# Normed tokens of the last six chunks written to DRAM and read back in squares of 32; VectorE transposes them instead of TensorE

## The chip, the core and the metric

The kernel runs on one core of a Trainium2 chip. The metric is the device time in microseconds of that core, as a median over runs. The profile shows one profiled execution.

## What is computed

The input is 2 sequences of 2048 tokens with 256 values each, all in float32. Two layers follow each other, each on normed tokens and added to its input:

```python
x = x + attention(layernorm(x))      # W_write, W_read, decay, log_alpha
x = x + mixture_of_experts(layernorm(x))

# attention: 4 heads of 64; causal, linear, with decay; the keys are the reads one token later
v  = y @ W_write.T;  rk = y;  wk = y moved down by one token
read = decay_part * (W_state @ rk) + ((rk @ wk.T) * M) @ v     # chunk by chunk
W_state = g_C * W_state + (v * g_w).T @ wk
out = y + (alpha * read) @ W_read.T

# experts: 8, the best 2 of each token by softmax, each 256 -> 1024 (gelu) -> 256
```

So a token of the attention is needed in three forms: normed, with tokens across the partitions (for the sums); transposed, with the 256 values across the partitions (`yT`, for the products); and moved by one token (`wk`, the keys).

## The kernel before, in words

**Chunks.** Each sequence is cut into 16 chunks of 128 tokens; a chunk holds both sequences. The attention walks over chunks p = 0 to 15 (`attention(p)`, here called pass p), each in seven steps with a yield between them. The order of instructions on every engine is the order in which this program writes them (a manual schedule); each engine runs its own list in order, SP (SyncE) too, which issues nearly all transfers. A transfer on SP that has to wait stops the transfers behind it.

**What a chunk passes through.** `norm_stats(p)` (L291) and `norm(p)` compute the normed tokens `y` two passes ahead: `norm(p + 2)` is the end of step 4 of pass p. Up to chunk 10 ACT writes `y` (L311), later VectorE (L315). Then `wk` is loaded from `y` on chip: its first row from the chunk before (L323), and the rest in two transfers of 112 and 15 rows (L324, L325). After that `load_x` (L98) asks for a later chunk of x. `transposes(p + 1)` stands in step 4 of pass p: four transposes by TensorE (L355) into the PSUM tile `pt` of 128x512, and a copy by ACT (L361) into `yT`, whose column 0 is the last token of the chunk before (L360). The tile `pt` shares its one PSUM buffer with `pK` of the routing (L627). Pass p itself opens with `pv` (L428) and `pS` (L437), which read `yT`; VectorE multiplies `pS` by the decay mask into `A` (L443), and `wk` by `g_w` into `wkg` (L382). Later in the pass come `pR` (L480, L488) with ACT's copy `rdT` (L493), then ACT's `sums` (L336), then `pW` (L508), which VectorE adds into the state (L513), then `rg` (L368) and `norm(p + 2)`. The result of the pass before (`pO`, L406, added by L409) is written by SP to `out` (L413).

**Experts beside it.** From pass 9 on, pieces of the second layer's work lie between the steps. A tile is 128 or 256 rows of one expert, and a piece is one eighth of its 1024 hidden values: `ph` (L894), gelu by ACT into `hT` (L899), and, three pieces later, `py` (L850). Which pieces stand after which step is fixed by `pieces_by`. `pv`, `pO`, `pW` and `ph` share three PSUM buffers of the tag "pm". A tile needs its rows `xg` from the slots in DRAM (L791, four transfers, in squares of 32 tokens), the numbers `wn` (L797), a bias `b2c` (L775) and 1 MB of weights `w1c` (L777); SP issues them one to three tiles ahead, with three buffers each (four for `b2c`). VectorE turns `xg` into `xT` by its transpose of squares of 32 (L821). At the end of a tile VectorE writes `yo` (L861) and POOL adds it to `out` (L864).

**Routing.** Every second pass a group of 512 tokens is routed in small VectorE instructions that are strewn between the others (L561 to L649), with four ACT instructions `payload` (L566) that need VectorE's shift (L252), two TensorE products `pK` (L627, L629), and POOL's writes of rows to the slots (L536).

Of the kernel before, what the change touches and what calls it, by code (L numbers as in the profile page):

```python
# [10 lines left out]
F32 = mybir.dt.float32  # L11
I32 = mybir.dt.int32
AF = mybir.ActivationFunctionType
ALU = mybir.AluOpType
# [4 lines left out]
P = 128  # L19
B, T, D = 2, 2048, 256  # L20
# [3 lines left out]
NC = T // P  # L24
# [6 lines left out]
S = 32  # L31
Q = P // S
# [28 lines left out]
def block_kernel(  # L61
# [12 lines left out]
    b2: bass.AP,  # L74
    out: bass.AP,
    slots: bass.AP,
):
    nc = tc.nc

# [2 lines left out]
    chk = ctx.enter_context(tc.tile_pool(name="chk", bufs=2))  # L82
# [13 lines left out]
    def load_x(p):  # L96
        xin = chk.tile([P, B, D], F32, tag="xin", name=f"xin_{p}", bufs=4)
        nc.sync.dma_start(xin, x.rearrange("b t d -> t b d")[p * P : (p + 1) * P])  # L98
        return xin
# [70 lines left out]
    g_w = one([P, H], F32, "g_w")  # L170
# [99 lines left out]
                return  # L270

    ys, wks, yTs, x1s, ups, stats2, rgs, wkgs = {}, {}, {}, {}, {}, {}, {}, {}
    shifts, vs, rdTs = {}, {}, {}
    EASY = 9
    BUSY = 8
    LATE = 7
    mark = {}
# [2 lines left out]
    def group_tiles(q):  # L280
        if q not in x1s:
            x1s[q] = grp.tile([P, G, D + E], F32, tag="x1", name=f"x1_{q}")
            stats2[q] = grp.tile([P, G, 2], F32, tag="mv2", name=f"mv2_{q}")
        return x1s[q], stats2[q]
# [13 lines left out]
    def norm(p):  # L298

        xin = xins[p]  # L300
        mv, ve, rstd = ups[p]
        shift = shift_of(mv[:, :, 0], rstd, B, f"a{p}")
        ups[p] = (mv, ve, rstd)
        beside()
        up = sml.tile([P, B], F32, tag="up", name=f"up_{p}")
        nc.vector.tensor_scalar(up, rstd, 1.0, None, ALU.add)
        shifts[p] = (shift, up)
        y = chk.tile([P, B, D], F32, tag="y", name=f"y_{p}", bufs=3)
        for b in range(B):
            if 1 < p < EASY + 2:  # L310
                nc.scalar.activation(  # L311
                    y[:, b, :], xin[:, b, :], AF.Identity, bias=shift[:, b : b + 1], scale=rstd[:, b : b + 1]
                )
            else:
                nc.vector.tensor_scalar(  # L315
                    y[:, b, :], xin[:, b, :], rstd[:, b : b + 1], shift[:, b : b + 1], ALU.mult, ALU.add
                )

        wk = chk.tile([P, B, D], F32, tag="wk", name=f"wk_{p}")
        if p == 0:  # L320
            nc.gpsimd.memset(wk[0:1, :, :], 0.0)
        else:
            nc.sync.dma_start(wk[0:1, :, :], ys[p - 1][127:128, :, :])  # L323
        nc.sync.dma_start(wk[1:113, :, :], y[0:112, :, :])  # L324
        nc.sync.dma_start(wk[113:128, :, :], y[112:127, :, :])  # L325
        ys[p], wks[p] = y, wk
        if p + 2 < NC:
            xins[p + 2] = load_x(p + 2)

    def sums(p):  # L330

# [17 lines left out]
    def transposes(p):  # L349

        yT = chk.tile([P, B, 2, P + 1], F32, tag="yT", name=f"yT_{p}")
        pt = ps_t.tile([P, B, 2, P], F32, tag="pt", name=f"pt_{p}")
        for b in range(B):
            for c in range(2):
                nc.tensor.transpose(pt[:, b, c, :], ys[p][:, b, c * P : (c + 1) * P], ident)  # L355
        if p == 0:
            nc.gpsimd.memset(yT[:, :, :, 0:1], 0.0)
            nc.vector.tensor_copy(yT[:, :, :, 1:], pt)  # L358
        else:
            nc.scalar.copy(yT[:, :, :, 0:1], yTs[p - 1][:, :, :, P : P + 1])  # L360
            nc.scalar.copy(yT[:, :, :, 1:], pt)  # L361
        yTs[p] = yT

    def scaled_reads(p):

# [7 lines left out]
    def scaled_writes(p):  # L373
        if p < NC - 1:
            wkg = chk.tile([P, B, H, HD], F32, tag="wkg", name=f"wkg_{p}", bufs=1)
            wk = wks[p].rearrange("p b (h d) -> p b h d", h=H)
            if p < EASY:
                for h in range(H):
                    nc.scalar.activation(wkg[:, :, h], wk[:, :, h], AF.Identity, scale=g_w[:, h : h + 1])
            else:  # L380
                for b in range(B):
                    nc.vector.tensor_tensor(  # L382
                        wkg[:, b], wk[:, b], g_w.unsqueeze(2).to_broadcast([P, H, HD]), ALU.mult
                    )
            wkgs[p] = wkg
# [32 lines left out]
    def attention(p):  # L418


        q, at = p // 2, 2 * (p % 2)
        first, last = p == 0, p == NC - 1
        x1, _ = group_tiles(q)
        yT = yTs[p]
        for b in range(B):
# [21 lines left out]
        beside()  # L447
        if p + 2 < NC and p < EASY:
            norm_stats(p + 2)
# [9 lines left out]
        if not last:  # L459
            transposes(p + 1)  # L460
        if p + 2 < NC and p >= EASY:
            norm_stats(p + 2)
# [21 lines left out]
        for b in range(B):  # L484
            for hh in range(2):
                for j in range(2):
                    hs = slice((2 * hh + j) * HD, (2 * hh + j + 1) * HD)
# [9 lines left out]
        for b in range(B):  # L497
            if p < EASY:
                nc.scalar.activation(x1[:, at + b, D:], vs[b][:, D:], AF.Identity, scale=std1[:, b : b + 1])
            else:  # L500
                nc.vector.tensor_scalar(x1[:, at + b, D:], vs[b][:, D:], std1[:, b : b + 1], None, ALU.mult)
        if not last:
            pW = ps_m.tile([P, B, 2, HD], F32, tag="pm", name=f"pW_{p}")
            for b in range(B):
                for hh in range(2):
                    for j in range(2):
                        h = 2 * hh + j
# [471 lines left out]
    for p in range(NC):  # L979
        for k, _ in enumerate(attention(p)):  # L980
            if p == 0 and k == 0:
                behind_first()
            if (p or k > 3) and k in (0, 2, 3, 4, 5) and halves < W2_BY[p]:
                e, j = divmod(halves, 2)
# [91 lines left out]
```

## Time and profile before

| | |
|---|---|
| median of 3 runs | 623.9 us (622.66 to 626.26) |
| the profiled execution's own time | 626.45 us |
| its span, first to last instruction | 624.7 us |
| mean granted TensorE clock | 0.990 |
| TensorE transposes, L355 | 64, of which 24 for chunks 10 to 15 |
| wk transfers, L323, L324, L325 | 15, 16 and 16 |
| TensorE starts on the transposes of chunks 10 to 15 | 103.65, 126.69, 150.83, 179.93, 210.39, 245.59 us |

The span is the time from the first to the last instruction of the program; the device time of the same execution is 1.7 us longer. A row of the timeline reads: start, duration, engine, line, operation, what it writes and reads, form, count, and in brackets the idle time of the engine before it and what ended it. Rows marked "q" are the engine's sequencer, which issues transfers; a transfer's row is the time of its issue, not of its landing. A row of a table by windows reads: stretch, its length, busy time and number of instructions of each engine, the granted TensorE clock as a share of full speed, the busy share of the 16 DMA engines, and GB/s. Matmuls are pipelined, so how long a group holds TensorE is read from the start of the next group. q1 is the queue of SP's transfers; its row gives packets, megabytes, and the share of the time of 16 DMA engines.

### The profile page before, as it was taken

The page shows a single profiled execution, that of the slowest core. Times are in us where ns is not written, and L with a number is a line of the kernel's source. Part 1 is how long each engine was busy: PE and PEld are TensorE (multiplying, and loading weights), DVE is VectorE, ACT ScalarE, POOL GpSimd, SP SyncE. Part 2 cuts the span into 40 slices and gives each one's busy share as a digit, 9 for nine tenths or more (in the row PEclk, how much of TensorE's full clock was granted, in tenths as well). Part 3 has the DMA queues.
Part 4 walks back from the last instruction along what each step waited for, and adds up shares of the span by engine and source line. Part 5 has one row for each costly group of instructions (what it writes and reads, how often), then busy time and mean ns, then how long its engine had stood idle before and what let it go on. Part 6 is the DMA issues. An engine that isn't in the chain of part 4 may idle for free. (4 is left out here: it accounts for less than half of the span.)

```text
span 624.7 us, 12845 instructions
## 1 busy us (share of the span) xinstructions
PE 603.0 (97%) x3864; PEld 529.3 (85%) x3864; DVE 249.3 (40%) x1039; ACT 240.7 (39%) x586; POOL 223.6 (36%) x199
## 2 busy tenths in 40 slices
PE   7998879999999999999999999999999999999995
PEld 6876758888888888888888888888888899999995
DVE  4787876567345534452255111221111132222220
ACT  6686673352333332422232222222222234444442
POOL 3216655546315622455266222222222121221121
PEclk9998998999999999999999999999999999999999
DMA  4799595679645366446657676466445568777742
GB/s 133 232 341 325 161 278 158 167 213 247 163 109 131 89 149 149 110 115 168 141 122 196 158 180 134 93 130 127 118 101 136 140 182 206 194 199 227 208 107 28
DMA packets 88856, 102.53 MB, mean 164 GB/s; under 512 B 52576, under 2 KB 77024, under 8 KB 83152
## 3 DMA queue, kind: packets, MB, share of 16 engines
q1 hardware_dynamic: 75360, 84.03, 46.8%
q0 software_dynamic: 12720, 17.47, 15.3%
q8 instruction: 35, 0.57, 0.4%
q14 instruction: 37, 0.30, 0.2%
q10 hardware_dynamic: 704, 0.14, 0.1%
HBM read 74.41 MB, written 23.01 MB: 156 GB/s over the span
## 5 line engine op out<-in xcount | busy, mean ns | idle before, releaser
L894 PE MATMUL ph<-xT,w1c 128*128 128x256 f32 (+1 forms) x1408 | 294.3, 332 | 5.7 <-issue 4.8
L850 PE MATMUL py<-w_sb,hT 128*128 x1072 | 288.8, 380 | 0.0
L899 ACT ACTIVATE hT<-ph,b1c 128x256 f32<-128x256 f32 (+1 forms) x352 | 148.4, 422 | 322.3 <-PE ph L894 293.6
L894 PEld LDWEIGHTS ph<-xT,w1c 128*128 128x128 f32 x1408 | 240.6, 192 | 34.6 <-issue 5.1
L864 POOL DMA_INDIRECT out<-yo,dest x67 | 105.2, 1570 | 291.1 <-DVE yo L861 196.1
L850 PEld LDWEIGHTS py<-w_sb,hT 128*128 128x128 f32 x1072 | 191.3, 191 | 19.2
L861 DVE SCALAR_TENSOR_TENSOR yo<-py,wt,b2c 128x256 f32<-128x256 f32 x67 | 30.3, 481 | 249.9 <-PE py L850 249.9
L536 POOL DMA_INDIRECT slots<-pay,slot_i x64 | 63.3, 989 | 62.2 <-issue 30.6
L428 PE MATMUL pv<-wwg,yT 128*128 128x264 f32 x128 | 33.9, 411 | 1.5 <-DVE yT L358 1.5
L406 PE MATMUL pO<-wrg,rdT 128*128 128x264 f32 x128 | 34.2, 401 | 0.0
L443 DVE TENSOR_TENSOR A<-pS,dmask 128x1024 f32<-128x1024 f32 x16 | 19.6, 1223 | 35.9 <-PE pS L437 28.8
L428 PEld LDWEIGHTS pv<-wwg,yT 128*128 128x128 f32 x128 | 24.4, 198 | 5.9 <-DVE yT L358 1.7
L406 PEld LDWEIGHTS pO<-wrg,rdT 128*128 128x128 f32 x128 | 24.0, 194 | 4.6 <-ACT v L430 0.2
L821 DVE STREAM_TRANSPOSE xT<-xg 128x512 f32<-128x512 f32 (+1 forms) x44 | 25.4, 576 | 0.2 <-issue 0.2
L836 DVE TENSOR_SCALAR b2c<-b2c,wt 128x256 f32<-128x256 f32 x67 | 23.8, 356 | 2.4
L409 DVE TENSOR_TENSOR x<-x,pO 128x264 f32<-128x264 f32 x32 | 13.4, 426 | 20.2 <-PE pO L406 20.2
L488 PE MATMUL pR<-A,v 128*64 128x128 f32 x256 | 18.0, 279 | 2.9 <-issue 2.2
L247 POOL TENSOR_TENSOR rstd_a<-ve_a,expo 128x2 f32<-128x2 f32 x16 | 11.6, 723 | 25.2 <-DVE ve_a L245 13.7
L566 ACT ACTIVATE pay<-x,shift_b,rstd_b 128x256 f32<-128x256 f32 x32 | 19.0, 593 | 3.8 <-DVE shift_b L252 3.7
L437 PEld LDWEIGHTS pS<-yT 64*128 64x128 f32 x256 | 15.5, 187 | 5.8 <-issue 3.7
L488 PEld LDWEIGHTS pR<-A,v 128*64 128x64 f32 x256 | 13.9, 136 | 6.0 <-issue 4.9
L437 PE MATMUL pS<-yT 64*128 64x128 f32 x256 | 18.6, 284 | 0.0
(161 smaller groups left out, 392.5 us busy)
## 6 DMA issues: line engine op xcount, KB each, us to landing
w1c<-in_w SPq DMA_DIRECT2D x44, 1024.0 KB
w_sb<-in_w SPq DMA_DIRECT2D x16, 512.0 KB
xg<-slots SPq DMA_DIRECT2D x92, 64.0 KB
b2c<-in_b SPq DMA_DIRECT2D x44, 128.0 KB
out<-x SPq DMA_DIRECT2D x16, 256.0 KB
xin<-in_x SPq DMA_DIRECT2D x15, 256.0 KB
wk<-y SPq DMA_DIRECT2D x16, 224.0 KB
xg<-slots SPq DMA_DIRECT2D x84, 32.0 KB
```

Source lines behind the costliest of these rows:

```text
L406: nc.tensor.matmul(pO, lhsT=rdTs[p][:, c, b * P : (b + 1) * P], rhs=wrg[:, c, :], start=(c == 0), stop=(c == 1))
L428: nc.tensor.matmul(pv, lhsT=yT[:, b, c, 1:], rhs=wwg[:, c, :], start=(c == 0), stop=(c == 1))
L437: nc.tensor.matmul(pS[:, j, (2 * b + hh) * P : (2 * b + hh + 1) * P], lhsT=yT[r, b, hh, 0:P], rhs=yT[r, b, hh, 1:], start=True, stop=True,)
L488: nc.tensor.matmul(pR[half(j, hh), hh, b * P : (b + 1) * P], lhsT=vs[b][:, hs], rhs=A[:, j, b, hh * P : (hh + 1) * P], start=(first and b ...
L536: put = nc.gpsimd.indirect_dma_start(out=next(slot_views), out_offset=IndirectOffsetOnAxis(ap=index, axis=0), in_=rows, in_offset=None,)
L821: nc.vector.transpose(xT.rearrange("p c (i s) -> p c i s", s=S), xg.rearrange("p i (c s) -> p c i s", s=S))
L836: nc.vector.tensor_scalar(b2c[:, j], b2c[:, 0], wt[:, j : j + 1], None, ALU.mult)
L850: nc.tensor.matmul(r["py"][:, j * D : (j + 1) * D], lhsT=hT[:, j * SB : (j + 1) * SB], rhs=w2_sb[:, ds(r["at"], 1), fc * D : (fc + 1) * D] ...
L861: nc.vector.scalar_tensor_tensor(yo, r["py"][:, j * D : (j + 1) * D], r["wt"][:, j : j + 1], r["b2c"][:, j], ALU.mult, ALU.add)
L864: add = nc.gpsimd.indirect_dma_start(out=next(out_views), out_offset=IndirectOffsetOnAxis(ap=r["dest"][:, j : j + 1], axis=0), in_=yo, in_ ...
L894: nc.tensor.matmul(ph, lhsT=r["w1c"][:, c, fc * P : (fc + 1) * P], rhs=r["xT"][:, c, :], start=(c == 0), stop=(c == 1),)
L899: mark[0] = nc.scalar.activation(hT, ph, AF.Gelu_apprx_tanh, bias=r["b1c"][:, fc : fc + 1]).ins.name
```

## The change

From chunk 10 on (the eleventh), `norm(p)` writes `y` with its 256 values in another order (squares of 32 interleaved), and SP writes it to a new DRAM tensor `normed`. At the start of the pass before the chunk's own, the new function `squares(p)` reads it back twice: as `wk`, rows 0 to 126 into partitions 1 to 127 in one transfer, and its first row from the chunk before (for chunk 10, in four small transfers from `y` of chunk 9 on chip); and as `yg`, in four transfers, one for each 32 partitions, so that each square of 32 tokens by 32 values lies where VectorE's transpose of squares turns it into its part of `yT`. `transposes(p)` then is two VectorE transposes of 128x256 instead of TensorE's four and ACT's copy. `yg` takes its buffers from the tag of `y`. `scaled_writes` reads `wk` in the new order, in four VectorE instructions of 128x128 instead of two of 128x256.

```diff
--- before.py
+++ after.py
@@ -74,6 +74,7 @@
     b2: bass.AP,
     out: bass.AP,
     slots: bass.AP,
+    normed: bass.AP,
 ):
     nc = tc.nc
 
@@ -270,8 +271,9 @@
                 return
 
     ys, wks, yTs, x1s, ups, stats2, rgs, wkgs = {}, {}, {}, {}, {}, {}, {}, {}
-    shifts, vs, rdTs = {}, {}, {}
+    shifts, vs, rdTs, ygs = {}, {}, {}, {}
     EASY = 9
+    SQUARE = 10
     BUSY = 8
     LATE = 7
     mark = {}
@@ -307,15 +309,21 @@
         shifts[p] = (shift, up)
         y = chk.tile([P, B, D], F32, tag="y", name=f"y_{p}", bufs=3)
         for b in range(B):
+            at = by_square(y[:, b]) if p >= SQUARE else y[:, b]
+            of = xin[:, b].rearrange("p (c k s) -> p c k s", c=2, s=S) if p >= SQUARE else xin[:, b]
             if 1 < p < EASY + 2:
                 nc.scalar.activation(
-                    y[:, b, :], xin[:, b, :], AF.Identity, bias=shift[:, b : b + 1], scale=rstd[:, b : b + 1]
+                    at, of, AF.Identity, bias=shift[:, b : b + 1], scale=rstd[:, b : b + 1]
                 )
             else:
                 nc.vector.tensor_scalar(
-                    y[:, b, :], xin[:, b, :], rstd[:, b : b + 1], shift[:, b : b + 1], ALU.mult, ALU.add
+                    at, of, rstd[:, b : b + 1], shift[:, b : b + 1], ALU.mult, ALU.add
                 )
 
+        ys[p] = y
+        if p >= SQUARE:
+            nc.sync.dma_start(normed[p].rearrange("(b t) d -> t b d", b=B), y)
+            return next_x(p)
         wk = chk.tile([P, B, D], F32, tag="wk", name=f"wk_{p}")
         if p == 0:
             nc.gpsimd.memset(wk[0:1, :, :], 0.0)
@@ -323,9 +331,37 @@
             nc.sync.dma_start(wk[0:1, :, :], ys[p - 1][127:128, :, :])
         nc.sync.dma_start(wk[1:113, :, :], y[0:112, :, :])
         nc.sync.dma_start(wk[113:128, :, :], y[112:127, :, :])
-        ys[p], wks[p] = y, wk
+        wks[p] = wk
+        next_x(p)
+
+    def next_x(p):
         if p + 2 < NC:
             xins[p + 2] = load_x(p + 2)
+
+    def by_square(t):
+
+        return t.rearrange("p (k c s) -> p c k s", c=2, s=S)
+
+    def squares(p):
+
+
+        wk = chk.tile([P, B, D], F32, tag="wk", name=f"wk_{p}")
+        nc.sync.dma_start(wk[1:P], normed[p].rearrange("(b t) d -> t b d", b=B)[: P - 1])
+        if p > SQUARE:
+            nc.sync.dma_start(wk[0:1], normed[p - 1].rearrange("(b t) d -> t b d", b=B)[P - 1 : P])
+        else:
+            for b in range(B):
+                for c in range(2):
+                    nc.sync.dma_start(
+                        by_square(wk[0:1, b])[:, c],
+                        ys[p - 1][P - 1 : P, b, c * P : (c + 1) * P].rearrange("p (k s) -> p k s", s=S),
+                    )
+        wks[p] = wk
+        yg = chk.tile([P, B * Q, 2, S], F32, tag="y", name=f"yg_{p}", bufs=3)
+        rows = normed[p].rearrange("(j s) (k d) -> s j k d", s=S, k=Q)
+        for k in range(Q):
+            nc.sync.dma_start(yg[k * S : (k + 1) * S].rearrange("p j c s -> p j (c s)"), rows[:, :, k, :])
+        ygs[p] = yg
 
     def sums(p):
 
@@ -349,6 +385,16 @@
     def transposes(p):
 
         yT = chk.tile([P, B, 2, P + 1], F32, tag="yT", name=f"yT_{p}")
+        yTs[p] = yT
+        if p >= SQUARE:
+            nc.scalar.copy(yT[:, :, :, 0:1], yTs[p - 1][:, :, :, P : P + 1])
+            yg = ygs.pop(p)
+            for b in range(B):
+                nc.vector.transpose(
+                    yT[:, b, :, 1:].rearrange("p c (i s) -> p c i s", s=S),
+                    yg[:, b * Q : (b + 1) * Q].rearrange("p i c s -> p c i s"),
+                )
+            return
         pt = ps_t.tile([P, B, 2, P], F32, tag="pt", name=f"pt_{p}")
         for b in range(B):
             for c in range(2):
@@ -359,7 +405,6 @@
         else:
             nc.scalar.copy(yT[:, :, :, 0:1], yTs[p - 1][:, :, :, P : P + 1])
             nc.scalar.copy(yT[:, :, :, 1:], pt)
-        yTs[p] = yT
 
     def scaled_reads(p):
 
@@ -377,6 +422,15 @@
             if p < EASY:
                 for h in range(H):
                     nc.scalar.activation(wkg[:, :, h], wk[:, :, h], AF.Identity, scale=g_w[:, h : h + 1])
+            elif p >= SQUARE:
+                for b in range(B):
+                    for c in range(2):
+                        hs = slice(2 * c, 2 * c + 2)
+                        nc.vector.tensor_tensor(
+                            wkg[:, b, hs].rearrange("p h (k s) -> p h k s", s=S),
+                            by_square(wks[p][:, b])[:, c].rearrange("p (h k) s -> p h k s", h=2),
+                            g_w[:, hs].unsqueeze(2).unsqueeze(3).to_broadcast([P, 2, 2, S]), ALU.mult,
+                        )
             else:
                 for b in range(B):
                     nc.vector.tensor_tensor(
@@ -420,6 +474,8 @@
 
         q, at = p // 2, 2 * (p % 2)
         first, last = p == 0, p == NC - 1
+        if SQUARE <= p + 1 < NC:
+            squares(p + 1)
         x1, _ = group_tiles(q)
         yT = yTs[p]
         for b in range(B):
...
```

## The prediction

> **What bounds the kernel now.** I read the page's busy times first, then the order of instructions on TensorE and on SP around the changed chunks, then the gaps of TensorE.
>
> ```profile
> PE 603.0 (97%) x3864; PEld 529.3 (85%) x3864; DVE 249.3 (40%) x1039; ACT 240.7 (39%) x586; POOL 223.6 (36%) x199
> ...
> PEclk9998998999999999999999999999999999999999
> ...
> q1 hardware_dynamic: 75360, 84.03, 46.8%
> ```
>
> TensorE is busy 97% of the span at nearly full clock; no other engine passes 40%. From 160 us on it has no idle time at all, so each microsecond of TensorE work removed there is one off the end, and each new stall is one on it. What one group of transposes is worth is read from starts, since ends overlap (timeline, TensorE):
>
> ```profile
> 179.06 1.03 PE L850 MATMUL py<-w_sb,hT 128*128 x4
> 179.93 0.60 PE L355 MATMUL pt<-ident,y 128*128 128x128 f32 x4
> 180.36 1.03 PE L894 MATMUL ph<-xT,w1c 128*128 128x256 f32 x4
> ```
>
> The four transposes hold TensorE for 180.36 - 179.93 = 0.43 us (109 ns each), not the 0.60 printed. A gap costs more than its length (timeline, then busy time by windows):
>
> ```profile
> 94.40 2.05 PE L894 MATMUL ph<-xT,w1c 128*128 128x128 f32 x8 [4.80 <-issue]
> ```
>
> ```profile
> 94.40:98.00 3.60, 3.60 (x12) 3.19 (x13) 2.28 (x13) 1.66 (x4) 3.60 (x2) 0.50 0.70 189
> ```
>
> After 4.80 us of idleness the next 3.6 us ran at a granted clock of 0.50 (column PEclk): another 1.8 us lost. SP's transfers around pass 10 (the attention of chunk 10, which must fetch chunk 11):
>
> ```profile
> 120.19 0.09 SPq L777 DMA_DIRECT2D w1c<-in_w  x1
> 122.27 0.47 SPq L777 DMA_DIRECT2D w1c<-in_w  x1
> 123.81 2.08 SPq L791 DMA_DIRECT2D xg<-slots  x4
> 126.08 1.77 SPq L797 DMA_DIRECT2D wn<-slots  x1
> 127.98 1.44 SPq L413 DMA_DIRECT2D out<-x  x1
> ```
>
> `squares(11)` will stand, in program order, between the wn of 126.08 and the out of 127.98, behind two 1 MB loads. By the trace's completion records the second of these is complete at 131.9 and the wn at 133.2. But TensorE transposed chunk 11 at 126.69, before SP would even have issued its read.
>
> **The change, part by part.** *Removed:* 6 x 4 transposes, 6 x 0.43 = 2.6 us of TensorE, all on the path. Six ACT copies of 0.585 us (L361), beside other work: nothing.
>
> *Added on VectorE:* 12 transposes; nearest row, L821 at 128x256, 436 ns: 0.8 us a chunk. `wkg` in four pieces instead of two of 418 ns: +0.3 us. The strided y writes have no row; nothing to +0.4 us, I take nothing, as float32 rows stay 128-byte runs. VectorE is busy 13.8 of 20 us at 120:140, so about 1.1 us a chunk lies in its idle time, if nothing makes it wait.
>
> *Queues.* SP issues per chunk: three wk transfers (0.57 + 0.54 + 0.90 us) become one write (0.45, as L98), a wk read, its first row (four small ones for chunk 10) and four yg reads (0.5 each, as L791). The chain write, next x, weights, read begins about 1.0 to 1.4 us earlier and is 3 us longer (4.5 at chunk 10) past the read; the xg, w1c behind it are used 8 us and more later, so that alone costs nothing. No POOL issue moves, but its adds wait for yo, which wait with VectorE. The write waits for y as L324 did; the read waits for it to land, about 2 us (out at 91.83 lands 94.1), always over by then.
>
> *The wk read.* It now moves 127 rows of 2 x 1 KB in one transfer, where the kernel before has 112 + 15. Row first: of q1's 75,360 packets, the data rows of the transfers listed on the page make 68,704; the 6,656 left are completion posts, and 417 SP transfers at 16 each would be 6,672. The 16 missing are one for each of the sixteen 15-row transfers: the rows set how many DMA engines a transfer uses. This trace can't say what 127 does. The Trainium skill, "DMA: Bandwidth & Descriptors", section "Why a DMA increments its semaphore by 16 and not by 1", can: the largest number up to 16 that divides the slowest dimension, and 127 rows go to one engine. Spread over 16 the read takes 254 x 46 ns / 16 = 0.7 us (46 ns is the trace's median for a 1 KB packet on q1); on one it takes 11.7 us (10.4 at the 24.9 GB/s that an engine moves when the share is 1.0; an estimate of 13 with POOL's packets of 102 ns between). And the engine is a queue: a sixteenth of each later transfer waits behind it, so yg too is complete only then. I take one engine, 11.7.
>
> *The new wait.* VectorE stops at its transposes until yg has landed (T). Behind it stand the statistics, gate factors, shift of the routing, the state update (L513), y of the next chunk. TensorE gets 3 buffers of tag "pm": pW takes one that L513 frees, so the third `ph` after pW waits for it; in pass 10 ACT waits too, as the first `payload` (L566) needs the shift (L252).
>
> Pass 9: SP reaches the slot at 97.1 (98.5 less 1.4). Data from 98.3, wk to 110.0, yg's 64 packets of 18 ns on that engine 1.2, completion 0.6: T = 111.8. VectorE's turn is 105.5. L513 ends T + 0.8 + 2.9 (L291 to L501) + 0.5 = 116.0; the third ph was due at 111.27 - 0.44 = 110.8. Stall 5.2, and 1.8 of clock: 7.0.
>
> Pass 10: y of chunk 11 is ready 1.5 later, 117.5. From there to the slot SP took 15.2 (112.6 to 127.9), less 1.0: 131.7; the weights before it are complete 4.0 on, 135.7; wk 11.7, yg 1.8: T = 149.2. ACT's gelu of the second piece after pW ends at T + 4.9 (transposes 0.8, L291 to L252 1.6, payload, rdT and sums 2.1, gelu 0.4); TensorE was due to need it at 134.69 - 0.9 + 7.0 = 140.8. Stall 13.3, and about 1.2 of clock, ACT being the limit at first: 14.5.
>
> Pass 11: y at T + 4.8 = 154.0; SP's chain 13.8 - 1.0: 166.8; weights complete 5.5 later, 172.3; wk and yg: T = 185.8. L513 ends T + 4.7 = 190.5; the third ph is due at 159.54 - 1.3 + 21.5 = 179.7. Stall 10.8 and 1.8: 12.6.
>
> Pass 12: T = 217.3 by the same steps, L513 at 220.5, the third ph due at 220.2: nil. Passes 13 and 14: SP reaches the slot 16 and 9 us ahead of the turn even now, and the third ph comes 10 us after it: nil, 1.6 us short of a stall in the last.
>
> Sum: 7.0 + 14.5 + 12.6 - 2.6 = 31.5 us; three gaps of the trace before (0.29, 0.56, 0.40 us at 111 to 156) should vanish in the stalls: 30.5. The profiled execution took 626.45 us (span 624.7), 2.5 above the median of 623.9; its rows carry over to the median: 623.9 + 30.5 = 654.
>
> **Rivals.** *1. The read is spread over 16 engines* (the split of 112 + 15 was for another reason). Then pass 9 has no stall (T = 103, turn 105.5). In pass 10 the read still stands behind the two w1c loads: complete 131.9 - 1.4, xg, wk, yg and completion 4.0: T = 134.5. Gelu at 139.4, due 133.8: 5.6, with clock 6.8. Pass 11 about 1. Net +5: 629, range 621 to 635. For it: nothing in the trace excludes it; against it, the rule and the missing posts. 0.20.
>
> *2. The waits stay hidden, not slower.* VectorE's wait costs nothing as long as yg of chunk 11 is complete by 133.8 - 4.9 = 128.9. That needs the read spread and the weights not in its way. Then the 2.6 us are kept, with the small gaps gone 3.5: 621. Against it: loads of that queue complete in order in the trace. 0.10.
>
> *3. VectorE becomes the bound* by its own work: 1.1 us a chunk against 6 idle of 20. It would show as A (L443) late; I give it no chance of its own.
>
> **How the numbers follow.** One engine: 0.70, 654, its own range 645 to 666 (11.7 between 10.4 and 13 three times over, SP's chains 1 us each). Half a per cent is 3.1 us, about what a measurement of this kernel can tell from no change. Slower: nearly all of 0.70 and two thirds of rival 1, 0.83. Faster: only rival 2 with the gaps too, 0.04. Same: 0.13. The range 626 to 668 leaves out the ends of the first case and the low third of rival 1, and rival 2.
>
> **What would show it.** The transposes of VectorE (new line, 12 of them, near 0.44 us) preceded by idle time ended by the yg transfer: about 6, 15, 13 us in passes 9 to 11, 6 in pass 12. TensorE idle before `ph` L894 (its new line) three times, 5 to 13 us, PEclk below 0.9 in those slices. Completion posts 15 fewer for each wk read. Wrong: wk complete within 2 us of its neighbours (rival 1), no new idle time on TensorE (rival 2), or stalls in passes 12 to 14, which would say that the wk transfers also hold up w1c and xg.

## The result, and the profile after

The changed kernel takes 659.92 us (median of four runs, 655.62 to 662.03) against 624.25 us for the kernel before on the same chip: a ratio of 1.0556, 95% interval 1.0513 to 1.0600, slower by 35.7 us. The profiled execution is the fastest of the four (655.62 us, span 653.9); against the profiled execution of before (626.45, span 624.7) it is 29.2 us longer, and it is this difference that the traces can account for.

From the page of the changed kernel: busy time by engine, the granted clock in 40 slices, the hardware DMA queue (packets, MB, share), and the group of the new transposes (busy, mean ns of one, idle before and what ended it):

```profile
PE 606.9 (93%) x3840; PEld 532.0 (81%) x3840; DVE 255.8 (39%) x1061; ACT 236.6 (36%) x580; POOL 224.5 (34%) x199
...
PEclk9999989786999799999999999999999999999999
...
q1 hardware_dynamic: 83962, 87.18, 45.6%
...
L393 DVE STREAM_TRANSPOSE yT<-yg 128x256 f32<-128x256 f32 x12 | 4.6, 425 | 62.7 <-DMA yg<-normed 62.7
```

TensorE still is the engine with the most work, but it is idle more often: it has 24 matmuls fewer, and 47 us without work where there were 22. No other engine has become busy: VectorE went from 249.3 to 255.8 us. The twelve transposes on VectorE themselves cost 4.6 us in all; ahead of them VectorE stood still for 62.7 us. The waits view of the same kernel (engine and line, what ended the wait: total us, times, longest) says who else stood:

```profile
DVE yT L393 <- DMA yg<-normed: 62.7, 6, 15.4
ACT pay L622 <- DVE shift_b L253: 34.2, 5, 16.1
PE ph L950 <- DVE state L569: 20.5, 2, 13.1
PE ph L950 <- DMA w1c<-in_w: 7.7, 1, 7.7
```

Six waits of VectorE, one a chunk; only two long ones of TensorE that are traced to them, and one for weights. The lines of before are L894 (ph, now L950), L513 (state, now L569), L566 (payload, now L622), L252 (shift, now L253), L777 (w1c, now L833) and L850 (py, now L906).

Why the squares (yg) are late is read from SP's timeline around pass 9 (start, duration of the issuing, line, transfer):

```profile
95.70 0.28 SPq L349 DMA_DIRECT2D wk<-normed  x1
96.03 9.06 SPq L355 DMA_DIRECT2D wk<-y  x4
105.20 4.34 SPq L363 DMA_DIRECT2D yg<-normed  x4
...
114.32 0.33 SPq L833 DMA_DIRECT2D w1c<-in_w  x1
```

The read of 127 key rows is issued at 95.70; by the completion records it has landed at 109.2, and the four yg reads at 110.1 to 111.1. For a stretch in which it runs nearly alone, the windows view shows how little moves (last two columns: mean busy share of the 16 DMA engines, GB/s):

```profile
104.30:106.10 1.80, 1.80 (x14) 1.54 (x13) 0.00 (x0) 1.50 (x4) 0.00 (x0) 1.00 0.08 25
```

A share of 0.08 is 1.3 engines of 16, at 25 GB/s. Each engine that took part in a transfer reports its end by a small packet, here called a completion post, and the records of these posts show where the squares stood. In pass 10 the slow read landed at 147.3. Fifteen of the sixteen posts of each yg came between 143.5 and 145.5, while it still ran; the sixteenth posts came at 147.7, 147.9, 148.1 and 148.3, one after the other right behind it. So only that part of the squares which shared the engine with the slow read was late, and VectorE has to wait for all of them. In pass 9, moreover, the four small copies of the first key row, 0.5 KB each, hold SP for 9.06 us and the squares 4.34, so that the w1c load of the next tile, issued at 103.07 before, now goes out at 114.32.

How a wait of VectorE becomes one of TensorE is read in pass 10, on three engines of the changed kernel. VectorE's timeline:

```profile
148.33 0.77 DVE L393 STREAM_TRANSPOSE yT<-yg 128x256 f32<-128x256 f32 x2 [15.42 <-DMA yg<-normed]
```

ScalarE's:

```profile
134.22 0.37 ACT L955 ACTIVATE hT<-ph,b1c 128x128 f32<-128x128 f32 x1 [0.67 <-PE ph L950]
150.69 0.60 ACT L622 ACTIVATE pay<-x,shift_b,rstd_b 128x256 f32<-128x256 f32 x1 [16.11 <-DVE shift_b L253]
```

TensorE's:

```profile
137.57 0.61 PE L950 MATMUL ph<-xT,w1c 128*128 128x128 f32 x4
138.01 0.60 PE L906 MATMUL py<-w_sb,hT 128*128 x2
151.69 1.19 PE L950 MATMUL ph<-xT,w1c 128*128 128x128 f32 x4 [13.08 <-DVE state L569]
```

The shift of the routing stands behind the transposes in VectorE's program, the payload waits for the shift, ScalarE's gelus stand behind the payload, and TensorE has two ph buffers to fill before it stops. It resumes at 151.69, 3.4 us after the squares were there.

Around this gap of pass 10 the granted clock was 0.50 (windows view of the changed kernel; the column before the last two is the granted clock):

```profile
143.50:157.10 13.60, 5.42 (x19) 4.91 (x20) 8.05 (x38) 4.92 (x12) 3.35 (x3) 0.50 0.34 85
```

An estimate of what that costs is half of TensorE's busy time in such stretches, here 2.7 us. Added up from 75 to 320 us, TensorE's time without work grew from 8.4 to 34.1 us (+25.7), the time lost at half clock by this estimate from 2.8 to 8.7 us (+5.9), and 24 transposes at 0.109 us are gone (-2.6): +29.0, against a span longer by 29.2.

### The profile page after: what moved, and what is told of

It reads as the page before. It is cut to its first block, busy times and chain, and to the rows that moved or that the text cites. A ratio compares the mean times of both kernels' runs of the same rounds, so it can differ in the third digit from the quotient of the medians.

```text
span 653.9 us, 12851 instructions
## 1 busy us (share of the span) xinstructions
PE 606.9 (93%) x3840; PEld 532.0 (81%) x3840; DVE 255.8 (39%) x1061; ACT 236.6 (36%) x580; POOL 224.5 (34%) x199
## 3 DMA queue, kind: packets, MB, share of 16 engines
q1 hardware_dynamic: 83962, 87.18, 45.6%
## 5 line engine op out<-in xcount | busy, mean ns | idle before, releaser
L950 PE MATMUL ph<-xT,w1c 128*128 128x256 f32 (+1 forms) x1408 | 297.5, 335 | 31.1 <-DVE state L569 20.5
L950 PEld LDWEIGHTS ph<-xT,w1c 128*128 128x128 f32 x1408 | 243.6, 194 | 61.8 <-issue 31.9
L906 PE MATMUL py<-w_sb,hT 128*128 x1072 | 292.2, 383 | 0.0
L955 ACT ACTIVATE hT<-ph,b1c 128x256 f32<-128x256 f32 (+1 forms) x352 | 148.3, 422 | 327.9 <-PE ph L950 303.0
L906 PEld LDWEIGHTS py<-w_sb,hT 128*128 128x128 f32 x1072 | 193.1, 193 | 19.5
L484 PE MATMUL pv<-wwg,yT 128*128 128x264 f32 x128 | 32.3, 396 | 2.4 <-DVE yT L393 1.6
L622 ACT ACTIVATE pay<-x,shift_b,rstd_b 128x256 f32<-128x256 f32 x32 | 19.0, 594 | 34.2 <-DVE shift_b L253 34.2
L393 DVE STREAM_TRANSPOSE yT<-yg 128x256 f32<-128x256 f32 x12 | 4.6, 425 | 62.7 <-DMA yg<-normed 62.7
L892 DVE TENSOR_SCALAR b2c<-b2c,wt 128x256 f32<-128x256 f32 x67 | 25.4, 378 | 2.4
```

Source lines behind the costliest of these rows:

```text
L484: nc.tensor.matmul(pv, lhsT=yT[:, b, c, 1:], rhs=wwg[:, c, :], start=(c == 0), stop=(c == 1))
L892: nc.vector.tensor_scalar(b2c[:, j], b2c[:, 0], wt[:, j : j + 1], None, ALU.mult)
L906: nc.tensor.matmul(r["py"][:, j * D : (j + 1) * D], lhsT=hT[:, j * SB : (j + 1) * SB], rhs=w2_sb[:, ds(r["at"], 1), fc * D : (fc + 1) * D] ...
L950: nc.tensor.matmul(ph, lhsT=r["w1c"][:, c, fc * P : (fc + 1) * P], rhs=r["xT"][:, c, :], start=(c == 0), stop=(c == 1),)
L955: mark[0] = nc.scalar.activation(hT, ph, AF.Gelu_apprx_tanh, bias=r["b1c"][:, fc : fc + 1]).ins.name
```

## The experiments

Each ratio is to the kernel before on the same chip, whose median was between 620.4 and 624.8 us from one set of runs to another; where an expectation names microseconds, it had about 624 in mind. Ratios are therefore the safer comparison. They come from the runs with their interval, and are not always the exact quotient of the two medians given.

| kernel | ratio to before, 95% interval |
|---|---|
| the change | 1.0556 (1.0513 to 1.0600) |
| keys read as 112 + 15 rows | 1.0110 (1.0069 to 1.0152) |
| keys read as 113 + 14 rows | 1.0529 (1.0469 to 1.0590) |
| squares read ahead of the keys | 1.0215 (1.0158 to 1.0271) |
| keys' read on ScalarE's queue | 1.0830 (1.0799 to 1.0861) |
| only the keys by DRAM | 1.0043 (1.0000 to 1.0086) |
| only the squares by DRAM | 1.0139 (1.0112 to 1.0166) |
| early reads, keys as 127 rows | 1.0273 (1.0244 to 1.0303) |
| early reads, keys as 112 + 15 | 1.0066 (1.0043 to 1.0089) |
| pW in another PSUM bank | 1.0543 (1.0499 to 1.0588) |
| the same and an early shift | 1.0526 (1.0500 to 1.0552) |
| early reads from the thirteenth chunk on | 0.9967 (0.9943 to 0.9990) |
| the same, only the squares by DRAM | 0.9945 (0.9918 to 0.9973) |

### One engine or sixteen: where the read is cut

```diff
-        nc.sync.dma_start(wk[1:P], normed[p].rearrange("(b t) d -> t b d", b=B)[: P - 1])
+        src = normed[p].rearrange("(b t) d -> t b d", b=B)
+        nc.sync.dma_start(wk[1:113], src[:112])
+        nc.sync.dma_start(wk[113:P], src[112 : P - 1])
```

> The changed kernel with one edit: the read of 127 key rows is cut into 112 and 15 rows, as the kernel before cuts its copy. If the single DMA engine of the 127-row read is the cause, the read takes under 2 us, the yg of chunk 11 lands near 134.5 instead of 148, VectorE waits some 6 us there and hardly at all in passes 9 and 12, and the time is near 629 us (621 to 635), some 30 below the changed kernel. If the way over DRAM itself (write, its landing, read in 256-byte rows) is the cause, the time stays above 650 us.

Measured: 631.22 us, ratio 1.0110. In pass 9 the read's parts have landed within 2.8 us of their issue, where 127 rows took 13.5. VectorE still waits 2.7, 9.1, 6.3, 2.3, 0 and 0 us, which is more than was expected. The second kernel moves the cut by one row, to 113 and 14:

> The same cut moved by one row: 113 and 14 rows. Under the divisor rule 113, a prime, goes to one engine: 226 packets of 46 ns, 10.4 us in a row, waits of VectorE as in the changed kernel less 1 to 2 us each, and 650 to 658 us. If it is the number of packets in one transfer or the mere lack of a cut that counts, it equals the cut of 112 and 15, near 629 us.

Measured: 656.0 us, ratio 1.0529. The same bytes in the same number of transfers, one row moved from one to the other, and 25 us or 4% apart. SP's timeline in pass 9 shows the difference, first with 112 + 15:

```profile
96.01 0.37 SPq L350 DMA_DIRECT2D wk<-normed  x1
96.44 0.50 SPq L351 DMA_DIRECT2D wk<-normed  x1
96.99 2.55 SPq L357 DMA_DIRECT2D wk<-y  x4
```

then with 113 + 14:

```profile
94.04 0.28 SPq L350 DMA_DIRECT2D wk<-normed  x1
94.37 5.82 SPq L351 DMA_DIRECT2D wk<-normed  x1
100.24 2.55 SPq L357 DMA_DIRECT2D wk<-y  x4
```

Behind 113 rows, the next transfer is held for 5.82 us; behind 112, for 0.50. The page counts the engines too, in the packets of q1. With 112 + 15:

```profile
q1 hardware_dynamic: 84142, 87.18, 47.3%
```

With 113 + 14:

```profile
q1 hardware_dynamic: 84046, 87.18, 45.9%
```

The data are the same 87.18 MB as in the changed kernel, so what differs from its 83,962 packets is completion posts: +180 is 6 x 30 and +84 is 6 x 14. With one post for each engine used, 127 rows give 1, 112 + 15 give 16 + 15 = 31, and 113 + 14 give 1 + 14 = 15: 30 and 14 more a chunk, to the packet. The read of 127 rows uses one engine.

### What stands behind the read

The squares are moved ahead of the keys' read in `squares`, nothing else:

```diff
     def squares(p):
+        yg = chk.tile([P, B * Q, 2, S], F32, tag="y", name=f"yg_{p}", bufs=3)
+        rows = normed[p].rearrange("(j s) (k d) -> s j k d", s=S, k=Q)
+        for k in range(Q):
+            nc.sync.dma_start(yg[k * S : (k + 1) * S].rearrange("p j c s -> p j (c s)"), rows[:, :, k, :])
+        ygs[p] = yg
         wk = chk.tile([P, B, D], F32, tag="wk", name=f"wk_{p}")
...
         wks[p] = wk
-        yg = chk.tile([P, B * Q, 2, S], F32, tag="y", name=f"yg_{p}", bufs=3)
...
-        ygs[p] = yg
```

> The changed kernel with the order of the reads turned: the four yg transfers are issued before the 127-row read. If the loss is VectorE's wait for yg behind that read, the waits shrink by 11 to 12 us each (to some 6 us in pass 10) and the time falls to 630 to 645 us; what is left is SP held by the read, with weights of tile 2 late by 7 to 8 us in pass 9 as in the changed kernel, and rival 1's stall in pass 10. If the loss were all VectorE's wait, it would be near 629; if it lies in the traffic as such, there is no change from 655 to 660.

Measured: 637.66 us, ratio 1.0215. VectorE waits 0, 7.4, 5.0, 1.1, 0, 0 us for its squares. The order alone takes back 3.4 of the 5.6% that the change costs; the first-row copies are still held (10.02 us in pass 9), but TensorE's wait for a w1c, expected to stay at 7 to 8 us, is 1.7.

Is it SP's queue that makes the others late, or the engine? The slow read is given to ScalarE's queue:

```diff
-        nc.sync.dma_start(wk[1:P], normed[p].rearrange("(b t) d -> t b d", b=B)[: P - 1])
+        nc.scalar.dma_start(wk[1:P], normed[p].rearrange("(b t) d -> t b d", b=B)[: P - 1])
```

> The change with the 127-row read issued by ScalarE's queue and nothing else altered. If the squares are late because SP stands in the issue behind the slow read (the queue): the squares are issued 12 us sooner, land while the slow read still runs, VectorE waits 2 to 9 us as with 112 and 15 rows, and the time is 630 to 640 us, unless ScalarE is held at its own issue. If they are late because their own packets on the one busy engine stand behind the 254 packets (the engine): they still land at the end of the slow read or after it, VectorE waits 8 to 15 us, and the time is 645 to 660 us.

Measured: 672.35 us, ratio 1.0830, slower than either side expected. VectorE stands 7.4, 17.1, 16.9, 15.2, 7.3 and 11.8 us ahead of its transposes. SP's timeline at the same place, first and last of the four small copies:

```profile
94.83 1.98 SPq L355 DMA_DIRECT2D wk<-y  x3
```

```profile
109.08 0.57 SPq L355 DMA_DIRECT2D wk<-y  x1
```

The first three are issued in 0.66 us each: with the slow read out of its own queue, SP is no longer held in the issue. That hold is a matter of the queue. But the fourth waits for the slow read itself, and so do others later (waits view, SP's queue):

```profile
SPq L363 <- DMA wk<-normed: 29.3, 2, 17.6
SPq L847 <- DMA wk<-normed: 16.1, 1, 16.1
SPq L351 <- DMA wk<-normed: 16.1, 1, 16.1
SPq L833 <- DMA wk<-normed: 15.5, 1, 15.5
SPq L355 <- DMA wk<-normed: 12.2, 1, 12.2
```

None of these transfers uses what the read brings. The program hands out eight completion semaphores to its transfers in turn, and one that comes by the read's semaphore again has to wait until the read has landed: 89 us of SP's time in all. Each of the six slow reads caused one such wait. In the changed kernel the same wait is 2.7 us for a yg and 2.8 for two xg. The squares were never issued while the slow read ran, so this kernel does not show them passing it. The small copies did pass: each of the first three has four completion posts, and the last of the four came at 101.2 to 101.6, while the slow read, from the other queue, landed at 109.1. In the changed kernel, with everything on SP's queue, these last posts came at 109.4 to 110.0, behind the read's landing at 109.2. So packets of another queue get in between on the busy engine, and packets of the same queue stand behind. Moving the read to another queue is no cure all the same, because of the semaphores.

### Each part alone

First only the keys: the kernel before, TensorE's transposes and all, with the shifted keys written to DRAM and read back in one transfer of 127 rows from the eleventh chunk on.

```diff
...
+        if p >= SQUARE:
+            nc.sync.dma_start(normed[p].rearrange("(b t) d -> t b d", b=B), y)
...
+            return
...
+    def keys(p):
+        wk = chk.tile([P, B, D], F32, tag="wk", name=f"wk_{p}")
+        nc.sync.dma_start(wk[1:P], normed[p].rearrange("(b t) d -> t b d", b=B)[: P - 1])
+        nc.sync.dma_start(wk[0:1], ys[p - 1][P - 1 : P])
...
+        if SQUARE <= p + 1 < NC:
+            keys(p + 1)
```

> The kernel before with the keys alone changed: y of chunks 10 to 15 written to DRAM, its 127 rows read back in one transfer; TensorE still transposes, in the plain order. If the late weights of pass 9 come from SP and the engine being held by the 127-row read, they come here too: one gap of 4 to 9 us before a ph, with a half-speed stretch behind it, 630 to 636 us. If nobody is hurt as long as no one waits for yg, it is 624 us.

Measured: 627.32 us, ratio 1.0043 (1.0000 to 1.0086). The slow read is there in full, and SP is held behind it as before:

```profile
98.55 6.95 SPq L342 DMA_DIRECT2D wk<-y  x1
```

But the time hardly moves, 0.4% with an interval that reaches down to none: here VectorE waits for no square, and no ph waits for a w1c; the chain on SP is shorter as well, with one first-row copy and no squares. In this kernel the slow read costs only what somebody waits for behind it, and not its own length.

Then only the squares: keys shifted by copies on the chip, as before.

```diff
...
+            nc.sync.dma_start(wk[1:113, :, :], y[0:112, :, :])
+            nc.sync.dma_start(wk[113:128, :, :], y[112:127, :, :])
...
     def squares(p):
-        wk = chk.tile([P, B, D], F32, tag="wk", name=f"wk_{p}")
-        nc.sync.dma_start(wk[1:P], normed[p].rearrange("(b t) d -> t b d", b=B)[: P - 1])
...
-        wks[p] = wk
```

> The change with the keys shifted by copies on the chip again (112, 15 and 1 rows, as in the kernel before) and only the squares by DRAM, at the change's own place. Theory: with no slow read in front the squares land in 5 to 8 us, as in the kernel with 112 and 15 rows or a little sooner; VectorE waits 0 to 6 us in the first three chunks, TensorE 0 to 5 us in pass 10: 621 to 629 us. Rival (writing the tokens and reading them back as 128-byte runs costs most of the 32 us by itself): 645 or more.

Measured: 629.21 us against 620.43, ratio 1.0139: above what was expected, which would be 1.008 at most. VectorE waits 0, 11.4, 5.3, 2.2, 0, 0 us. Its interval overlaps that of 112 + 15 rows (1.0110), so the keys' round trip, once spread, costs nothing that these runs can tell; what is left, 1.1 to 1.4%, comes with the squares read at this place. In this kernel's trace two gaps of TensorE in pass 10 stand for it: 5.2 us for the state, behind a VectorE that waited for squares, and 4.2 us for a w1c load.

### The reads moved earlier

Now the reads stand one step after the norm of their own chunk, in the pass before, with the squares ahead of the keys:

```diff
-        if SQUARE <= p + 1 < NC:
-            squares(p + 1)
...
         if p + 2 < NC:
             norm(p + 2)
         yield
+        if SQUARE <= p + 2 < NC:
+            squares(p + 2)
         yield
         yield
```

Once with the read of 127 rows left whole:

> The same early place and squares ahead of the keys, but the read of 127 rows left whole. Theory of two costs (a wait for the squares, and SP held in the issue of what follows the slow read): the squares are ahead of the read, so VectorE waits 0 to 2 us; SP is still held 7 to 10 us a chunk at the first-row copy, so a w1c load behind it lands late in some passes: 623 to 632 us. If only the wait for the squares counts: 621 to 623. If the place does not matter (the slow read delays whatever comes): 638 or more, as with the squares first at the change's own place (637.7).

Measured: 637.14 us, ratio 1.0273. VectorE waits for squares 3.4 us in all, and still the loss is 2.7%, more than the two-cost theory gave and as much as the third case did, though not by its way: the squares are no longer what is late. SP's timeline, at the reads for chunk 10:

```profile
93.63 0.35 SPq L354 DMA_DIRECT2D wk<-normed  x1
94.03 9.30 SPq L360 DMA_DIRECT2D wk<-y  x4
104.64 2.80 SPq L847 DMA_DIRECT2D xg<-slots  x4
```

and what VectorE then waited for (waits view):

```profile
DVE xT L877 <- DMA xg<-slots: 36.9, 6, 12.5
```

The tokens of the next tile (xg) took the squares' place as what is late; TensorE stood 9.0 us, from 100.5 to 109.5, until VectorE had one of these tiles transposed.

And once with 112 + 15 rows:

> The change with three things altered: the 127-row read of the keys cut into 112 and 15 rows, the squares read ahead of the keys, and all of these reads issued one step after the norm of their own chunk, that is some 30 us earlier, ahead of the weight loads of the later steps. Theory (the read of 127 rows is slow because one DMA engine moves it, and what it costs is only VectorE's wait for squares that are issued too late): VectorE waits 0 us at all six chunks, no ph of TensorE waits over 1 us for a state or a w1c, and what is left is the 24 transposes taken off TensorE, -2.6 us: 620 to 623 us. Rival (the round trip by DRAM costs by itself, by holding SP or by its traffic): 624 to 632 us, with weights landing late.

Measured: 624.39 us against 620.43, ratio 1.0066: the rival. VectorE waits 4.0 us for squares, once. But the ten issues of SP ahead of xg take from 91.79 to 97.21, and TensorE has a new gap (its timeline):

```profile
102.60 0.68 PE L952 MATMUL ph<-xT,w1c 128*128 128x128 f32 x4 [2.80 <-issue]
```

Just before it, at 102.06, VectorE's xT began after 6.2 us for xg. With 1.6 us for a w1c in pass 10, and half of 3.4 us at half clock, that is 6.1 us lost against 2.6 gained: +3.5, of the 4.0 measured. This is no full account: it holds only the new gaps, and the profiled execution (623.16 us) happens to be shorter than that of the kernel before (626.45), which has small gaps of its own that are missing here.

### By which way VectorE's wait reaches TensorE

pW is given the PSUM bank of TensorE's transposes, which from then on only the routing's pK uses:

```diff
-            pW = ps_m.tile([P, B, 2, HD], F32, tag="pm", name=f"pW_{p}")
+            pool, tag = (ps_t, "pt") if p + 1 >= SQUARE else (ps_m, "pm")
+            pW = pool.tile([P, B, 2, HD], F32, tag=tag, name=f"pW_{p}")
```

> The change with one thing altered: from pass 9 on, pW is put into the PSUM bank of TensorE's transposes (free by then) in place of a buffer of the tag pm. It asks by which way VectorE's waits reach TensorE. VectorE's own waits for the squares stay as they are (10 to 15 us in passes 9, 10, 11 and 12). If they reach TensorE by pW's buffer alone: the two waits of a ph for the state (13.1 us in pass 10, 7.4 us in pass 12) go with the half clock behind them, and the time falls to 633 to 640 us. If the next pass's pv, which needs the transposed tokens, stands behind as a second barrier: TensorE runs some 8 us further and then waits for yT, and the time falls to 645 to 653 us only. If neither: 656 to 662 us.

Measured: 657.96 us, ratio 1.0543: the third case, nothing gained. TensorE's two waits stayed, under another name (waits view):

```profile
PE ph L951 <- ACT hT L956: 22.1, 2, 13.0
```

and in ScalarE's timeline of pass 10 the hT stand behind the payload:

```profile
148.44 0.60 ACT L623 ACTIVATE pay<-x,shift_b,rstd_b 128x256 f32<-128x256 f32 x1 [15.49 <-DVE shift_b L253]
```

So the buffer that the trace of the changed kernel names, pW's, was only the one of two causes that came last. With that bank kept, the small shift is also put ahead of the transposes in VectorE's program:

```diff
         yield
+        shift2 = shift_of(mv2[:, :, 0], rstd2, G, f"b{q}")
         yield
         yield
...
-        shift2 = shift_of(mv2[:, :, 0], rstd2, G, f"b{q}")
```

> The kernel with pW in the other PSUM bank, and with VectorE's small shift_b (L253), from which ScalarE's payload (L622) is made, moved ahead of the transposes of the squares on VectorE. With pW's bank alone the two long waits of TensorE stayed at 13.0 and 9.2 us, now for ScalarE's hT: in passes 10 and 12, and in no other, ScalarE's first payload waits 15.5 and 13.6 us for shift_b, which stands behind the waiting transposes, and the gelus stand behind it. Theory: VectorE's wait for squares reaches TensorE by two ways, ScalarE's payload and pW's buffer, and only both taken away bring it down: VectorE still waits 12 to 15 us in these passes, ScalarE's payload waits under 3 us, TensorE's two waits fall to 2 to 8 us (the next pass's pv then waits for yT), and the time is 638 to 650 us. If a third barrier stands at the same place: 654 to 660 us.

Measured: 653.01 us against 620.56, ratio 1.0526, its interval overlapping that of the change: the third barrier. The payload waits no more (0.0 us in passes 10 and 12). In pass 12 TensorE's wait splits into three (1.3, 2.7 and 1.3 us, from 7.4 in the change); in pass 10 it does seven pieces of ph where it did two, and then stands at the routing's own product (its timeline):

```profile
142.51 0.60 PE L907 MATMUL py<-w_sb,hT 128*128 x2
154.91 0.62 PE L684 MATMUL pK<-both,before 128*128 128x40 f32 x2 [11.79 <-DVE both L662]
```

This is a third way, through VectorE's one-hot tile `both`. (pK also shares its bank with pW in this kernel, so that without `both` it would still have had to wait until VectorE had read pW, at 150.7.) Behind a VectorE that stands 13.6 us, several of its outputs are late at once; the wait that the profile names is the last of them.

### From the thirteenth chunk on

The early version lost in passes 9 and 10; in the trace of before TensorE has no gap from 160 us on. The early version with 112 + 15 rows was therefore begun two chunks later:

```diff
-    SQUARE = 10
+    SQUARE = 12
```

> The early reads with 112 and 15 rows again, from the thirteenth chunk on in place of the eleventh (four chunks in place of six). The early version lost in passes 8 to 10, where SP's reads put the tiles' tokens and weights off by some 2.5 us; by the passes of chunks 12 to 15 the tiles have a longer stock, and TensorE has no gap. Theory: what is left is 16 transposes at 0.11 us taken off TensorE, -1.7 us, a ratio of 0.996 to 0.999 to the kernel before. Rival (each round trip costs time wherever it stands): a ratio of 1.002 to 1.006.

Measured: 622.75 us against 624.83, ratio 0.9967 (0.9943 to 0.9990): 2.1 us faster, where 16 transposes at 0.109 us make 1.7. VectorE waits 0.0 us at all four chunks. And with the keys by copies on the chip:

> The same from the thirteenth chunk on, but with the keys shifted by copies on the chip, so that only the squares go by DRAM. If the keys' way does not matter once the reads are early and cut in 112 and 15 rows: the same as the kernel with both by DRAM within 0.2 per cent, a ratio of 0.996 to 0.999. If the keys' reads still cost: 0.2 to 0.5 per cent faster than that kernel.

Measured: 621.83 us, ratio 0.9945 (0.9918 to 0.9973), faster than the kernel before. Against the one with both by DRAM (0.9967) the intervals overlap, so neither case of the expectation is settled.

## Why the prediction was right, and where its steps were not

It said 654 (own range of the likeliest case 645 to 666); 659.92 was measured. The cause was right; the sum came out close partly because errors in its terms made good for each other.

| pass | squares there (T), predicted, measured | VectorE's wait, predicted, measured | TensorE's loss with clock, predicted, measured |
|---|---|---|---|
| 9 | 111.8, 111.3 | 6, 9.8 | 7.0, 11.2 |
| 10 | 149.2, 148.3 | 15, 15.4 | 14.5, 15.8 |
| 11 | 185.8, 185.1 | 13, 12.6 | 12.6, 0.7 |
| 12 | 217.3, 214.0 | 6, 15.3 | 0, 9.8 |
| 13, 14 | none given, 245.3 and 281.4 | none given, 3.4 and 6.2 | 0, 0 |

T as measured is the start of VectorE's transposes. The measured losses are the gaps before a matmul plus half of the working time at half clock behind them (3.7, 5.4 and 4.8 us in passes 9, 10 and 12).

**The keys' read on one engine: right.** This step carried the forecast. The trace of before had one hint, 16 missing posts at the 15-row transfers; the Trainium skill ("DMA: Bandwidth & Descriptors", section "Why a DMA increments its semaphore by 16 and not by 1") gives the rule, the largest number up to 16 that divides the slowest dimension. The runs here agree with it: 112 + 15 against 113 + 14 rows, and the packet counts 30 and 14 a chunk apart. The size was right as well: predicted 11.7 us at 46 ns a packet; from issue to landing 13.5 us in pass 9, with 1.2 of start and 0.6 of completion in the prediction's own sum. That a part of each yg stands behind the read on its engine, and is complete only then, was right too: the sixteenth posts show it. And rival 1 is what the kernel with 112 + 15 rows does: T = 134.5 in pass 10 and a stall of 5.6 us were given for it, 134.3 and 6.8 were measured, at +5 against +6.5 us.

**T of the squares: right within 1 us in passes 9 to 11, and 3.3 too late in pass 12.** That SP's next transfer would be held 7 to 12 us was not in it. T came out right all the same, as the squares landed right behind the read; the weights did not.

**"That alone costs nothing", of the xg and w1c behind the read: wrong in pass 9.** SP's chain was put at 4.5 us longer for chunk 10; the first-row copies alone took 9.06, and the fourth yg, on the read's own completion semaphore, was issued only at 109.23, as the read landed. The w1c load went out 11.3 us later than before. TensorE's timeline:

```profile
122.68 1.20 PE L950 MATMUL ph<-xT,w1c 128*128 128x128 f32 x4 [7.72 <-DMA w1c<-in_w]
```

This, and not L513, is the loss booked to pass 9, whose reads caused it; it falls at the first ph of pass 10. The squares' own part was 1.6 us, at pass 10's pv. The prediction had named a stall in passes 12 to 14 as the sign that the reads hold up w1c and xg; the hold-up showed here instead.

**"The third ph after pW waits for it": wrong.** In pass 9 seven pieces of ph, in pass 11 six, ran between pW and the state that frees its buffer. TensorE's timeline of pass 11 has pW at 174.76, the state came at 188.88, and in between:

```profile
184.06 1.03 PE L950 MATMUL ph<-xT,w1c 128*128 128x256 f32 x4
185.78 1.94 PE L484 MATMUL pv<-wwg,yT 128*128 128x264 f32 x8
```

The other two buffers were enough here, where ScalarE emptied them. A wait of 12.6 us on VectorE then cost 0.7 on TensorE. Passes 10 and 12 have the routing's payload, which stops ScalarE for 16.1 and 13.5 us; passes 9 and 11 have none. The prediction had it in pass 10 (right: 14.5 against 15.8) and overlooked it in pass 12, where it comes again, as a group of routing is two chunks long. But the payload is not the whole of pass 12's miss. The third ph was put due at 220.2 there with the 12.6 us of pass 11 in it; by these times the payload alone would have cost some 2 us (an estimate: 217.3 + 4.9 against 220.2). TensorE had not lost these 12.6 us and ran out of work at 209.8, while the squares came only 3.3 us sooner than predicted: most of the time spared in pass 11 was lost in pass 12. The kernel with pW in another bank showed that taking its buffer away alone gains nothing even where the trace names it.

**The sum.** Predicted stalls were 34.1 us, measured ones 37.5: 11.9 too much in pass 11 made good most of the 9.8, 4.2 and 1.3 too little in passes 12, 9 and 10. Passes 11 and 12 belong together, as just said; that the rest came out so near is luck. The small gaps that were to vanish (1.0) are part of 5.9 us by which the profiled execution lost less elsewhere than that of before, more than half of it at one gap near 90 us, 4.8 us before and 2.2 here, and at the half clock behind it. In the profiled executions of the other kernels this gap is anything from 1.8 to 5.0 us, so this part seems to belong to the execution and not to the change. So the difference of the medians (+35.7) lies above that of the profiled executions (+29.2), and further from the forecast of +30.5.

**No stall in passes 13 and 14, TensorE's 2.6 us, VectorE's work hidden: right.** The kernel from the thirteenth chunk on shows the gain by itself, 2.1 us for 16 transposes with an interval that holds the 1.7 worked out.

## What to carry to other kernels

Before a transfer is reshaped, look at the number of its rows: 127 or 113 rows went over one DMA engine (25 GB/s moved in all while 127 did), 112 and 15 over sixteen and fifteen, and whatever was issued behind it, or shared its completion semaphore, was late by up to the length of the slow one. A round trip through DRAM must be started where its landing has slack, and what it pushes back on the issuing queue has to have slack as well: the same edit was 5.6% slower, 0.7% slower and 0.3% faster with its reads whole and late, split and early, and split, early and in a part with a stock of work. When an engine in the middle waits, follow each of its outputs to its consumer before trusting the one wait that the profile names: two such waits removed brought nothing that these runs can tell, since the next stood at the same place.

## What the runs showed of the hardware that was not expected

In these kernels, SP's next transfer behind the read on one engine stays in its issue until about half of that read's packets are through. In passes 9 to 12 of the changed kernel this issue ended at 103.24, 141.84, 178.31 and 207.26 us, and the read landed at 109.2, 147.3, 184.1 and 212.9: 5.5 to 6.0 us later (6.7 in pass 14; for pass 13 the trace lacks the landing). The packet records say how much was left. In pass 9 of the changed kernel 119 of the read's 254 packets had still to start when the issue ended; with the early read of 127 rows it was 118 of 254, with 113 rows 116 of 226. So the hold ended at about the same number left, whether 254 or 226 had stood there at first, and was shorter with fewer (7.2 and 5.8 us). With the slow read on ScalarE's queue, SP's next transfers took 0.66 us. That suggests a limit on how many packets may stand before one engine in one queue; what sets it, no run shows.

The completion semaphores are a second way in which one slow transfer holds others that have nothing to do with it: waits of 12 to 18 us on SP in the kernel with the read on ScalarE's queue.

The number of DMA engines that a transfer uses can be read from the page's packet count alone: at equal bytes, one completion post more for each engine more, 180 and 84 packets for six chunks.
